# Layer 0 of a two-layer image network: another form for three small VectorE steps in the running maximum over k

## The chip, the cores and the metric

The kernel runs on one core of one Trainium2 chip. The metric is device time in microseconds of one execution, start to end; the median of 3 runs before the change is 9257.32 us (9255.66 to 9263.38). Five engines work side by side on a core, each through its own queue in order: TensorE (PE, with its weight loads shown apart as PEld), VectorE (DVE), ScalarE (ACT), GpSimd (POOL) and SyncE (SP), which here only issues DMAs. Working memory is SBUF, matmul results land in PSUM, both with 128 partitions.

## The reference, cut to what matters

Layer 0 is a linear attention over the pixels of each of 8 images (128 x 128 pixels, 128 channels, 4 heads of 32). Its softmax of k runs over the pixels, all 16384 of them, and so needs a maximum over the pixels for each channel:

```
qkv = einsum('bhwc,cf->bhwf', x, w_qkv);  q, k, v = split(qkv, 3, axis=-1)
q, k, v = (t.reshape(B, 4, 32, N) for t in (q, k, v))       # the raw reshape of the reference
q = softmax(q, axis=-2) * 32 ** -0.5
k = softmax(k, axis=-1)
context = einsum('bhdn,bhen->bhde', k, v)
attn = einsum('bhde,bhdn->bhen', context, q)
out = attn.reshape(B, H, W, 128) @ w_out + b_out
x = layernorm(out) * gamma + beta + x
```

Layer 1 (a gated projection, a depthwise convolution, and a selective scan in four directions) takes layer 0's output and is not touched.

## The kernel before, in words

Layer 0 takes the first 2100 us or so. An image lies in SBUF with channels on partitions. It is worked off in 32 groups of 4 x 128 pixels, and a step of the loop in `image` carries one group through every stage. Two images are in work at once: `attend(b)` computes the output of image b, while `context(b + 1)` builds the 128 x 128 context matrix of the next one. The order of the calls in `image` (the list of `at(stage, t - lag)` calls) is the order of instructions on every engine: the whole layer is built under `in_order`, which chains each instruction to the one before it on its engine. The first pass (b = -1) has only a context, the last (b = 7) only an attend.

The maximum is kept as a running one, as in a flash attention. Four groups make a block (BK = 4), so an image has 8 blocks, j = 0 to 7:

- `key` (L180, L182): PE computes k of a group as a [128 pixels of a column, 4 x 128 channels] tile, ACT copies it to `k`.
- `larger` (L186 to L197): DVE keeps the elementwise maximum of the block's four groups in `run` (L190, L192: one operand is in PSUM). At the block's last group two more operations fold the 4 columns of `run` into its first one (L196, L197: both operands in SBUF).
- `fold` (L199 to L214), one step later: PE turns the folded column (L206), DVE reduces it to the maximum per channel, `m` [128, 1] (L208). From the second block on, `m` is raised to the one before it (L210) and the difference `a` = old minus new is formed (L212). Then the diagonal matrix `dg` = ident x m is made (L214).
- `spread` (L219, L221): PE multiplies `ones` with `dg`, which puts the maxima on every partition in `pmx`; ACT takes exp of `a`.
- `subtract`, `raise_to`, `add`: k minus maximum (L231), exp (L234), and the product with v (L240), summed over a block in `pc`; L247 rescales `total` by `a` and adds the block.

Around these stand the stages of `attend`: on DVE the maxima of q (L270), the subtraction (L272), the sums (L280), their reciprocals (L281), the addition of the bias (L296) and the variance sums (L302); on POOL the multiplication of q (L282), three operations of the layer norm (L308, L310, L313) and the residual addition (L327); on ACT the activations L275, L290, L298, L325; on PE the matmuls L268, L288, L294, L321. Per step DVE's order is: L272, L231, L280, L281, then the block-end work of `fold` (L208 to L214) where it falls, then L190 or L192 with L196 and L197 where they fall, L296, L302, L270. POOL's is: L308, L310, L313, L327, L282.

The pools: `sm` holds the small tiles with 4 buffers, `wp` the group tiles with 2 unless said otherwise (`run` has 2), `ps` six PSUM banks.

Of the kernel before, what the change touches and what calls it, by code (L numbers as in the profile page):

```python
# [8 lines left out]
F32 = mybir.dt.float32  # L9
BF16 = mybir.dt.bfloat16  # L10
AF = mybir.ActivationFunctionType
ALU = mybir.AluOpType
AX = mybir.AxisListType
# [3 lines left out]
P = 128  # L17
# [60 lines left out]
def layer0(ctx: ExitStack, tc, xT, w_qkv, w_out, b_out, gamma, beta, win, x1, zs):  # L78
# [12 lines left out]
    nc = tc.nc  # L91
    const = ctx.enter_context(tc.tile_pool(name="l0c", bufs=1))
    wp = ctx.enter_context(tc.tile_pool(name="l0w", bufs=2))
    sm = ctx.enter_context(tc.tile_pool(name="l0s", bufs=4))
# [3 lines left out]
    ident = const.tile([P, P], F32, name="ident")  # L98
# [40 lines left out]
    def group(b, g):  # L139
        return xs[b % 2][:, g * GW : (g + 1) * GW, :]  # L140
# [33 lines left out]
    def context(b):  # L174

        ks, pks, ms, runs, scales = {}, {}, {}, {}, {}

        def key(g):
            pk = ps.tile([P, GW, P], F32, name="pk", tag="ps")
            nc.tensor.matmul(pk, wq[:, P : 2 * P], group(b, g), start=True, stop=True)  # L180
            ks[g] = k = wp.tile([P, GW, P], F32, name="k", tag="k", bufs=7)
            nc.scalar.copy(k, pk)  # L182
            pks[g] = pk

        def larger(g):
            pk = pks.pop(g)  # L186
            j, i = divmod(g, BK)
            if i == 1:
                runs[j] = run = wp.tile([P, GW, P], F32, name="run")
                nc.vector.tensor_tensor(run, pk, ks[g - 1], ALU.max)  # L190
            elif i > 1:
                nc.vector.tensor_tensor(runs[j], pk, runs[j], ALU.max)  # L192

            if i == BK - 1:
                run = runs[j]
                nc.vector.tensor_tensor(run[:, 0:2], run[:, 0:2], run[:, 2:4], ALU.max)  # L196
                nc.vector.tensor_tensor(run[:, 0], run[:, 0], run[:, 1], ALU.max)  # L197

        def fold(g):  # L199

            j, i = divmod(g, BK)
            if i < BK - 1:
                return
            run = runs.pop(j)
            turned = ps.tile([P, P], F32, name="pmt", tag="ps")
            nc.tensor.transpose(turned, run[:, 0, :], ident)  # L206
            ms[j] = m = sm.tile([P, 1], F32, name="m")
            nc.vector.tensor_reduce(m, turned, AX.X, ALU.max)  # L208
            if j:
                nc.vector.tensor_tensor(m, m, ms[j - 1], ALU.max)  # L210
                scales[j] = a = sm.tile([P, 1], F32, name="a")
                nc.vector.tensor_tensor(a, ms.pop(j - 1), m, ALU.subtract)  # L212
            runs[j] = dg = sm.tile([P, P], F32, name="dg", bufs=2)
            nc.vector.tensor_scalar(dg, ident, m, None, ALU.mult)  # L214

        def spread(g):
            j, i = divmod(g, BK)
            if i == BK - 1:
                nc.tensor.matmul(pm[:, j % 2, :], ones, runs.pop(j), start=True, stop=True)  # L219
                if j:  # L220
                    nc.scalar.activation(scales[j], scales[j], AF.Exp)  # L221

        def value(g):
            pv = ps.tile([P, GW, P], F32, name="pv", tag="ps")
            nc.tensor.matmul(pv, wq[:, 2 * P : 3 * P], group(b, g), start=True, stop=True)
            nc.scalar.copy(vts[g % 3][:, :, 0:P], pv)

        def subtract(g):

            mb = pm[:, g // BK % 2 : g // BK % 2 + 1, :]  # L230
            nc.vector.tensor_tensor(ks[g], ks[g], mb.to_broadcast([P, GW, P]), ALU.subtract)  # L231

        def raise_to(g):
            nc.scalar.activation(ks[g], ks[g], AF.Exp)  # L234

        def add(g):
            k = ks.pop(g)
            j, n = divmod(g, BK)
            for i in range(GW):
                nc.tensor.matmul(  # L240
                    pc, k[:, i, :], vts[g % 3][:, i, :],
                    start=(n == 0 and i == 0), stop=(n == BK - 1 and i == GW - 1),
                )
            if n < BK - 1:
                return
            if j:
                nc.vector.scalar_tensor_tensor(total, total, scales.pop(j), pc, ALU.mult, ALU.add)  # L247
            else:
                nc.vector.tensor_copy(total, pc)
            if g == NG - 1:  # L250
                rs = sm.tile([P, 1], F32, name="rs")
                nc.vector.reciprocal(rs, total[:, P : P + 1])
                for h in range(NH):
                    s = slice(HD * h, HD * h + HD)
                    nc.vector.tensor_scalar(
                        ctxs[b % 2][s, s], total[s, s], rs[s, :], HD**-0.5, ALU.mult, ALU.mult
                    )

        return key, larger, fold, spread, value, subtract, raise_to, add

    def attend(b):
# [1008 lines left out]
```

## Time and profile before

| what | before |
|---|---|
| median of 3 runs | 9257.32 us |
| the profiled execution, its own time | 9261.02 us |
| its span in the profile | 9259.2 us |
| layer 0, first context alone | about 0 to 110 us |
| layer 0, passes b = 0 to 6 (attend and context together) | about 110 to 2100 us |
| in 900 to 1200 us: PE busy | 276.63 us of 300 |
| in 900 to 1200 us: DVE busy | 209.68 us of 300 |
| in 900 to 1200 us: ACT, POOL busy | 179.65 us, 153.13 us of 300 |

A group in the profile is one line of the kernel on one engine: how often it ran, its total busy time, its mean duration, and the idle time of the engine just before it, with what ended that idle time. A line of a timeline gives start, duration, engine, source line and tiles of one instruction. A matmul in float32 is two passes in the records (x2). DVE's records may overlap by some 0.08 us[...].

### The profile page before, as it was taken

How to read it: one execution, taken by the hardware profiler on the slowest of the kernel's cores; microseconds unless marked ns; L12 is line 12 of the kernel's file. 1: busy time of each engine (PE TensorE's matmuls, PEld its weight loads, DVE VectorE, ACT ScalarE, POOL GpSimd, SP SyncE). 2: the span in 40 equal slices, each digit the busy share in tenths (PEclk: the TensorE clock that was granted, in tenths of full speed). 3: DMA queues.
4: the chain of work that ended last, by engine and by line, in shares of the span. 5: the costliest groups of instructions: out<-in, count | busy, mean ns of one | idle time of the engine just before them, and what ended most of it. 6: DMA issues, size and time to landing. Idle time of an engine off the chain costs nothing. (4 is left out here: it accounts for less than half of the span.)

```text
span 9259.2 us, 91316 instructions
## 1 busy us (share of the span) xinstructions
PE 6337.5 (68%) x24512; PEld 3096.6 (33%) x24512; DVE 7992.0 (86%) x7953; ACT 7099.7 (77%) x8066; POOL 7316.5 (79%) x4684
## 2 busy tenths in 40 slices
PE   8899998988899999999434636446364463643636
PEld 5555555554333333333101304114031140311403
DVE  6667666774699999999799999999999999999996
ACT  5555555657789999999688887887878888888885
POOL 3446444554588988888599899998999989999897
PEclk9999999999999999999655757557575575755857
DMA  1322333123478789888758769587695876957767
GB/s 76 146 84 96 137 121 146 70 109 137 148 242 249 251 246 244 245 246 241 206 154 238 208 185 258 158 230 216 179 260 159 222 225 178 257 165 218 230 174 211
DMA packets 934769, 1750.66 MB, mean 189 GB/s; under 512 B 150228, under 2 KB 376148, under 8 KB 926064
## 3 DMA queue, kind: packets, MB, share of 16 engines
q1 hardware_dynamic: 873328, 1509.92, 49.4%
q0 software_dynamic: 60928, 234.90, 13.8%
q8 instruction: 200, 3.28, 0.1%
q14 instruction: 313, 2.56, 0.1%
HBM read 1052.36 MB, written 692.12 MB: 188 GB/s over the span
## 5 line engine op out<-in xcount | busy, mean ns | idle before, releaser
L951 POOL TENSOR_TENSOR h<-ubt,sp 128x1024 f32<-128x1024 f32 x1024 | 2422.4, 2399 | 348.4 <-ACT mv L1058 124.1
L934 PE MATMUL px<-rows,dtw 128*128 128x512 bf16 x2048 | 953.5, 565 | 2266.2 <-DVE y L1001 1084.5
L534 DVE SCALAR_TENSOR_TENSOR acc<-xb,cw,acc 128x1024 f32<-128x1024 f32 x1024 | 1320.3, 1289 | 133.7 <-ACT xb L502 89.9
L526 POOL TENSOR_TENSOR tap<-tap 128x1024 f32<-128x1024 f32 x512 | 1224.0, 2394 | 243.9 <-ACT tap L524 220.6
L938 ACT ACTIVATE sp<-px 128x1024 f32<-128x1024 f32 x1024 | 1047.3, 1024 | 435.4 <-PE px L934 418.1
L961 DVE TENSOR_TENSOR_SCAN h<-px,h 128x1024 f32<-128x1024 f32 x512 | 1177.3, 2331 | 31.7 <-ACT px L942 15.1
L934 PEld LDWEIGHTS <-dtw 128*128 128x128 bf16 x2048 | 169.1, 110 | 3089.1 <-issue 1022.7
L959 DVE TENSOR_TENSOR_SCAN h<-px,h 128x1024 f32<-128x1024 f32 x512 | 1177.9, 2330 | 21.4 <-POOL h L951 18.8
L1009 POOL TENSOR_TENSOR y<-y,h 128x512 f32<-128x512 f32 x768 | 1159.8, 1559 | 3.8 <-DVE h L982 3.8
L942 ACT ACTIVATE px<-sp,sa 128x1024 f32<-128x1024 f32 x1024 | 1110.4, 1109 | 6.1
L515 PE MATMUL acc<-xi,wt 128*128 128x512 f32 x2048 | 938.3, 601 | 53.7 <-ACT ures L539 53.7
L524 ACT ACTIVATE tap<-xb,cw 128x1024 f32<-128x1024 f32 x768 | 837.3, 1139 | 15.2 <-POOL xb L499 15.1
L282 POOL TENSOR_TENSOR q<-q,qs 128x512 f32<-128x512 f32 x256 | 272.2, 1063 | 695.5 <-DVE qs L281 695.5
L938 ACT ACT_TABLE_LOAD x512 | 656.9, 1283 | 170.0 <-PE px L934 168.0
L942 ACT ACT_TABLE_LOAD x512 | 656.9, 1283 | 9.1
L1074 PEld LDWEIGHTS px<-wg,z 128*128 128x128 f32 x4096 | 575.3, 225 | 114.8 <-issue 109.1
L1074 PE MATMUL px<-wg,z 128*128 128x128 f32 x4096 | 574.7, 308 | 0.0
L967 PE MATMUL pc<-rows,csel 128*128 128x512 bf16 x1024 | 517.5, 586 | 78.2 <-DVE rstd L1062 74.5
L515 PEld LDWEIGHTS acc<-xi,wt 128*128 128x128 f32 x2048 | 375.1, 189 | 574.4 <-issue 411.9
L488 PE MATMUL pxb<-xi,wi 128*128 128x512 f32 x1024 | 496.2, 607 | 2.1 <-ACT xb L497 2.1
L298 ACT ACTIVATE sq<-o 128x512 f32<-128x512 f32 x256 | 161.2, 630 | 421.0 <-DVE o L296 419.8
L1001 DVE TENSOR_TENSOR y<-y,px 128x1024 f32<-128x1024 f32 x384 | 468.6, 1220 | 14.4
(153 smaller groups left out, 15038.8 us busy)
## 6 DMA issues: line engine op xcount, KB each, us to landing
ubt<-ubs SPq DMA_DIRECT2D x1024, 512.0 KB
zs<-z SPq DMA_DIRECT2D x512, 256.0 KB
ubs<-ures SPq DMA_DIRECT2D x256, 512.0 KB
ubs<-turned SPq DMA_DIRECT2D x256, 512.0 KB
z<-zs SPq DMA_DIRECT2D x256, 512.0 KB
y<-gs POOLq DMA_DIRECT2D x128, 1024.0 KB, 10.3
gs<-du POOLq DMA_DIRECT2D x96, 1024.0 KB, 8.6
rows<-xps SPq DMA_DIRECT2D x1536, 60.0 KB
```

Source lines behind the costliest of these rows:

```text
L515: nc.tensor.matmul(acc[:, s, :], wt[:, j, c, :], x, start=(j == 0), stop=(j == len(ON_PE) - 1))
L524: nc.scalar.activation(t, at(n, c, *d), AF.Copy, scale=weight(n, c, *d))
L526: nc.gpsimd.tensor_tensor(sums[n, c], sums[n, c], t, ALU.add)
L534: nc.vector.scalar_tensor_tensor(acc, at(n, c, *d), weight(n, c, *d), acc, ALU.mult, ALU.add)
L934: nc.tensor.matmul(p[:, hf * 512 : hf * 512 + 512], sl.dw[:, c * P : c * P + P], src, start=True, stop=True)
L938: nc.scalar.activation(t, da[n, c], AF.Softplus)
L942: nc.scalar.activation(da[n, c], sp[n, c], AF.Exp, scale=sa[:, sl.s, c : c + 1])
L951: nc.gpsimd.tensor_tensor(h, u, t, ALU.mult)
L959: nc.vector.tensor_tensor_scan(e[:, ::-1], x[:, ::-1], e[:, ::-1], start, ALU.mult, ALU.add)
L961: nc.vector.tensor_tensor_scan(e, x, e, start, ALU.mult, ALU.add)
L1009: nc.gpsimd.tensor_tensor(v[:, c], v[:, c], h[:, c], ALU.add)
L1074: nc.tensor.matmul(po[:, w, :], z[:, c, w * H : w * H + H], wg[:, c, :], start=(c == 0), stop=(c == NC2 - 1))
```

## The change

The two tensor operations at the end of `larger` become one reduction over the four columns: it reads `run` in the order "p h w", so that the four values to be compared lie 128 elements (512 bytes) apart, and writes a tile of its own, `top`. The transposition in `fold` then reads `top`. The maximum and the difference of `fold` become tensor-scalar operations, whose second operand is the [128, 1] tile taken as a scalar per partition; the values are the same.

```diff
             if i == BK - 1:
                 run = runs[j]
-                nc.vector.tensor_tensor(run[:, 0:2], run[:, 0:2], run[:, 2:4], ALU.max)
-                nc.vector.tensor_tensor(run[:, 0], run[:, 0], run[:, 1], ALU.max)
+                runs[j] = top = sm.tile([P, P], F32, name="top", bufs=2)
+                nc.vector.tensor_reduce(top, run.rearrange("p w h -> p h w"), AX.X, ALU.max)
 
         def fold(g):
...
-            run = runs.pop(j)
+            top = runs.pop(j)
             turned = ps.tile([P, P], F32, name="pmt", tag="ps")
-            nc.tensor.transpose(turned, run[:, 0, :], ident)
+            nc.tensor.transpose(turned, top, ident)
             ms[j] = m = sm.tile([P, 1], F32, name="m")
             nc.vector.tensor_reduce(m, turned, AX.X, ALU.max)
             if j:
-                nc.vector.tensor_tensor(m, m, ms[j - 1], ALU.max)
+                nc.vector.tensor_scalar(m, m, ms[j - 1], None, ALU.max)
                 scales[j] = a = sm.tile([P, 1], F32, name="a")
-                nc.vector.tensor_tensor(a, ms.pop(j - 1), m, ALU.subtract)
+                nc.vector.tensor_scalar(a, ms.pop(j - 1), m, None, ALU.subtract)
             runs[j] = dg = sm.tile([P, P], F32, name="dg", bufs=2)
             nc.vector.tensor_scalar(dg, ident, m, None, ALU.mult)
```

## The prediction

> **What bounds the kernel now.** I read the page first: the span, the engines' shares, and the slices. Layer 0 is the first nine of the 40 slices.
>
> ```profile
> span 9259.2 us, 91316 instructions
> ...
> PE   8899998988899999999434636446364463643636
> ...
> DVE  6667666774699999999799999999999999999996
> ```
>
> PE is nearly full there and DVE far from it, so time comes off only where PE stands idle, and DVE counts where PE waits for it. The list of waits between 100 and 2100 us has, as PE's longest wait for another engine's arithmetic:
>
> ```profile
> PE pmx L219 <- DVE dg L214: 49.0, 46, 1.3
> ```
>
> PE waits for `dg`, the last product of the fold that is changed, about 1.07 us in each of 46 cases. Next, the instructions of the tiles `run` and `m` (minimum/median/maximum in ns):
>
> ```profile
> L196 DVE TENSOR_TENSOR run<-run x64: 424/1140/1516, 22.2 to 2081.1; 128x256 f32<-128x256 f32 x64
> L197 DVE TENSOR_TENSOR run<-run x64: 291/292/1020, 22.6 to 2082.7; 128x128 f32<-128x128 f32 x64
> ```
> ```profile
> L208 DVE TENSOR_REDUCE m<-pmt x64: 227/228/291, 23.4 to 2085.6; 128x1 f32<-128x128 f32 x64
> L214 DVE TENSOR_SCALAR dg<-ident,m x64: 272/274/570, 23.8 to 2086.2; 128x128 f32<-128x128 f32 x64
> L210 DVE TENSOR_TENSOR m<-m x56: 158/504/514, 33.7 to 2085.9; 128x1 f32<-128x1 f32 x56
> L212 DVE TENSOR_TENSOR a<-m x56: 158/970/972, 33.9 to 2086.1; 128x1 f32<-128x1 f32 x56
> ```
>
> An operation on one element per partition takes 158 ns or 970. The timelines of DVE, POOL and PE around one fold show what makes the difference:
>
> ```profile
> 1054.31 0.23 DVE L208 TENSOR_REDUCE m<-pmt 128x1 f32<-128x128 f32 x1
> 1054.57 0.50 DVE L210 TENSOR_TENSOR m<-m 128x1 f32<-128x1 f32 x1
> 1055.11 0.97 DVE L212 TENSOR_TENSOR a<-m 128x1 f32<-128x1 f32 x1
> 1056.00 0.28 DVE L214 TENSOR_SCALAR dg<-ident,m 128x128 f32<-128x128 f32 x1
> 1056.20 0.68 DVE L296 TENSOR_TENSOR o<-po,bb 128x512 f32<-128x512 f32 x1
> ```
> ```profile
> 1053.79 1.27 POOL L327 TENSOR_TENSOR x<-x1t,x 128x512 f32<-128x512 f32 x1
> 1055.01 1.05 POOL L282 TENSOR_TENSOR q<-q,qs 128x512 f32<-128x512 f32 x1
> ```
> ```profile
> 1053.88 1.16 PE L321 MATMUL pt<-d,o 128*128 128x128 f32 x8
> 1056.33 0.49 PE L219 MATMUL pmx<-dg,ones 128*128 128x128 f32 x2 [1.28 <-DVE dg L214]
> ```
>
> L210 ends with POOL's L327 (1055.07 against 1055.06), L212 with L282 (1056.08 against 1056.06). While these hold DVE, PE idles. L196 does the same a step earlier: it starts 0.19 us after an L282 and ends after it.
>
> [...] L196 to L212 wait, while the SBUF reduction L280 has a mean of 686 ns beside the same POOL work. [...] no row here shows a one-element tensor-scalar. L214 (128 elements, source in SBUF) [...] in first blocks, where it follows L208 directly, it takes 570 ns.
>
> **The change part by part.**
>
> *Folding the columns.* Out go L196 and L197. In 48 of the 56 blocks with POOL at work, L196's start to L296's start is 1.38 to 1.41 us, in each image's last block 1.75, so I take 1.39. In comes a reduction of 512 elements. Contiguous it would be 0.69 us (L280). But its reads hop 512 bytes at each element. The nearest row hops the same way:
>
> ```profile
> L152 DVE COPY v<-x x192: 637/749/1566, 341.5 to 1867.0; 128x512 f32<-128x512 f32 x192
> ```
>
> [...] L296 starts 0.08 us before the end of the operation ahead of it, at 1.06. Gain 0.33 per block (bounds 0.04 and 0.78). In the first pass POOL is idle and the pair takes 0.75 us together; the reduction loses 0.4 there, 8 times, beside PE's own matmuls: nothing to 3 us.
>
> *Maximum and difference.* 42 folds (blocks 1 to 6 of 7 passes) have both blocked; block 0 has neither, block 7 finds POOL free. A tensor-scalar with a pointer: [...] 0.206 us for one element (bounds 0.158, the tensor form, and 0.215). From L208's start: maximum at 0.26 to 0.47, difference (a gap of 0.04, as between L210 and L212) at 0.51 to 0.71, L214 0.08 before its end, at 0.63. [...] L327's record ends at 0.75, L282's begins at 0.70. [...] Each image's first block has a like case: L196 starts at 1022.78, L282 at 1022.84, and L196 runs its full-speed 0.42 while L282 stretches to 1.28. So 0.06 us ahead is enough; 0.19 behind isn't. L214 would be 0.07 ahead[...]. I take that L214 wins: end at 0.90, L296 at 0.83 instead of 1.89, a gain of 1.06 per fold. If it loses, [...] L296 at 1.76: a gain of 0.13. In block 7 and the first pass the fold becomes 0.1 longer (14 times, 1 us at most).
>
> *Other edits.* `top` instead of `run` for the transposition: same size, its step comes later than the fold, PE waited 2.9 us in all for it. `run` is free earlier; nobody waits for it. No DMA and no queue is moved.
>
> **The sum.** Starts of L196 are 26.16 us apart in most blocks (1414.19, 1440.35, 1466.51). DVE's saving there would be 0.33 + 1.06 = 1.39. But PE sets a floor: its query matmuls are 6.12 us apart in steps without a fold (1056.65, 1062.77), so a block takes 4 x 6.12, plus 0.11 for the transposition and 0.32 for L219: 24.91. So at most 1.25 per block is saved, and what is late next is PE itself. 42 x 1.25 = 52.5; blocks 0 and 7 give about 0.25 each, 14 x 0.25 = 3.5. Sum 56 us. The profiled execution took 9261.02 (span 9259.2), 3.7 above the median of 9257.32; from the median, 9257.3 - 56 = 9201. Layer 1 has the same instructions.
>
> **The rivals.**
>
> *A, forecast: L214 gets in before L282.* 9201. With the reduction at its dear end 1.10 per block remain: 46 + 1, so 9210; with all at its best the floor holds at about 9196.
>
> *B: L214 loses to L282.* The wait moves from L212 to L214. 42 x (0.33 + 0.13) + 3.5 = 23, so 9234; with the reduction at either bound 9248 to 9216. For it: the near tie. Against it: the 0.06 us case.
>
> *C: the change doesn't do what it says, since the one-element forms wait too.* L210 and L212 stay as long as before. 42 x 0.33 + 3.5 = 17, so 9240. For it: tensor-scalars of 128 elements wait, and no row shows one element. [...]
>
> *D, slower: the strided reduction costs more than what it replaces.* With B holding too, it decides from 1.39 + 0.08 + 0.13 = 1.60 us on, 2.8 ns per hop. [...] 2.15 us, 42 x 0.55 + 14 x 0.6 = 31 us slower, 9288. Against it: [...] the reductions L280 and L302 cost the same 686 ns with rows of 32 and of 128, so short rows add nothing visible.
>
> **How the numbers follow.** A 0.55, B 0.23, C 0.15, D 0.07. About 0.2% (18.5 us) is what a measurement of this kernel can tell from no change. A is faster by more; of B and C, at 23 and 17 us, about half: 0.19. So faster 0.74, within 0.2% 0.19, slower 0.07. The range reaches from A's best, with some of PE's remaining waits for POOL's `d` taken too, 9190, over B and C to 9246.
>
> **What would show it.** The reduction's row: 1.14 us, the same with and without POOL at work. L210 and L212: about 0.21 in all 56. L214: 0.27 with L282 stretched (A), or about 1.2 (B). PE's wait for `dg` nearly gone (A) or about 0.5 to 0.8 per fold (B, C). Distance of blocks: 24.9 (A), 25.7 (B), 25.8 (C), over 26.2 (D). I am wrong if the one-element forms wait, if the hop costs over 2.8 ns, or if PE turns out to have a floor above 24.9.

## The result and the profile after

The median after is 9187.98 us (9182.95 to 9194.06), against 9256.49 before in the runs that were taken beside it: 68.5 us less, ratio 0.9926 with a 95% interval of 0.9914 to 0.9939. That is faster, as forecast, but the forecast was 9201 (56 us less), and the time lies 2 us below the range of 9190 to 9246.

The page of the changed kernel, with the same lines as before:

```profile
span 9182.9 us, 91090 instructions
...
PE   8999999998899999999334536345363463643636
...
DVE  6667666673899999999799999999999999999996
```

PE's slices of layer 0 read 9 more often, DVE's hardly changed: what went away was idle time of PE. PE's list of waits from 100 to 2100 us (total, cases, longest) has the old wait nearly at the end:

```profile
PE pt L321 <- POOL d L313: 30.9, 32, 1.9
...
PE pmx L219 <- DVE dg L214: 0.6, 4, 0.2
```

49.0 us before, 0.6 now. The wait for POOL's `d`, at the starts of the images, is now the longest on arithmetic. The instructions that write `top` and `m` (minimum/median/maximum, ns; first that of `top`, then, from the view of the other tile, those of `m`):

```profile
L197 DVE TENSOR_REDUCE top<-run x64: 1018/1056/1072, 23.1 to 2013.1; 128x128 f32<-128x512 f32 x64
```
```profile
L208 DVE TENSOR_REDUCE m<-pmt x64: 226/228/292, 24.6 to 2016.8; 128x1 f32<-128x128 f32 x64
L214 DVE TENSOR_SCALAR dg<-ident,m x64: 274/277/568, 25.0 to 2017.5; 128x128 f32<-128x128 f32 x64
L210 DVE TENSOR_SCALAR m<-m x56: 211/214/216, 35.2 to 2017.1; 128x1 f32<-128x1 f32 x56
L212 DVE TENSOR_SCALAR a<-m x56: 211/214/215, 35.5 to 2017.3; 128x1 f32<-128x1 f32 x56
```

None of the three new forms waits anywhere, with POOL at work or without: minimum and maximum lie 4 to 54 ns apart. One fold on the timelines of DVE and POOL:

```profile
1050.57 0.23 DVE L208 TENSOR_REDUCE m<-pmt 128x1 f32<-128x128 f32 x1
1050.83 0.21 DVE L210 TENSOR_SCALAR m<-m 128x1 f32<-128x1 f32 x1
1051.08 0.21 DVE L212 TENSOR_SCALAR a<-m 128x1 f32<-128x1 f32 x1
1051.21 0.27 DVE L214 TENSOR_SCALAR dg<-ident,m 128x128 f32<-128x128 f32 x1
1051.40 0.68 DVE L296 TENSOR_TENSOR o<-po,bb 128x512 f32<-128x512 f32 x1
```
```profile
1050.04 1.28 POOL L327 TENSOR_TENSOR x<-x1t,x 128x512 f32<-128x512 f32 x1
1051.27 1.12 POOL L282 TENSOR_TENSOR q<-q,qs 128x512 f32<-128x512 f32 x1
```

`dg` starts 0.06 us before L282 and runs unhindered; L282 takes 1.12 us instead of 1.05, longer by 0.07 us. L296 follows L208 after 0.83 us, where it was 1.89. So in all 42 folds.

The time can be followed step by step on DVE by the distance from one variance sum (L302) to the next, the median over the 7 passes, in us:

| step | before | after |
|---|---|---|
| with the column fold, blocks 1 to 6 | 7.39 | 6.98 to 7.08 |
| with the rest of the fold (next step) | 6.99 | 5.94 |
| each of the two others | 5.89 | 5.89 |
| column fold of block 0 | 7.16 | 6.72 |
| column fold of block 7 | 6.45 | 5.67 |

For example, the step with the rest of a fold, before and then after (6.99 and 5.94 us apart):

```profile
1077.08 0.69 DVE L302 TENSOR_REDUCE var<-sq 128x4 f32<-128x512 f32 x1 [0.76 <-ACT sq L298]
1084.07 0.69 DVE L302 TENSOR_REDUCE var<-sq 128x4 f32<-128x512 f32 x1 [0.76 <-ACT sq L298]
```
```profile
1046.90 0.69 DVE L302 TENSOR_REDUCE var<-sq 128x4 f32<-128x512 f32 x1 [0.76 <-ACT sq L298]
1052.84 0.69 DVE L302 TENSOR_REDUCE var<-sq 128x4 f32<-128x512 f32 x1 [0.76 <-ACT sq L298]
```

A pass from its first L302 to its last takes 199.5 us before and 189.8 after (sum of the seven: 68.2 us less). The first L302 of all comes 2.2 us later (122.5 to 124.7: the first pass got longer), and the stretches between passes add up to 2.7 less. The last L302 starts at 2084.4 before and 2015.6 after: 68.8 us, the whole result. The profiled executions differ by 76.3 us (9261.02 and 9184.71), 7.5 more than layer 0 gives. What follows layer 0 has the same instructions in all kernels here, yet in their profiled executions it took from 7167 to 7187 us. So below, "end of layer 0" is the start of the last L302 (or of the same instruction under a shifted line number), and small effects are read from it.

### The profile page after: what moved, and what is told of

It is laid out like the page before. It is cut to its first block, busy times and chain, and to the rows that moved or that the text cites. A ratio compares the mean times of both kernels' runs of the same rounds, so it can differ in the third digit from the quotient of the medians.

```text
span 9182.9 us, 91090 instructions
## 1 busy us (share of the span) xinstructions
PE 6273.2 (68%) x24350; PEld 3080.2 (34%) x24512; DVE 7929.7 (86%) x7889; ACT 7102.3 (77%) x8066; POOL 7317.2 (80%) x4684
## 5 line engine op out<-in xcount | busy, mean ns | idle before, releaser
L934 PE MATMUL px<-rows,dtw 128*128 128x512 bf16 x1893 | 909.9, 573 | 2302.7 <-DVE y L1001 1084.5
L282 POOL TENSOR_TENSOR q<-q,qs 128x512 f32<-128x512 f32 x256 | 273.0, 1066 | 694.6 <-DVE qs L281 691.1
L938 ACT ACT_TABLE_LOAD x512 | 656.9, 1283 | 169.5 <-PE px L934 122.8
L982 DVE TENSOR_TENSOR h<-h,pc 128x1024 f32<-128x1024 f32 x384 | 466.0, 1214 | 0.0
```

The costliest lines, as they stand in the source:

```text
L934: nc.tensor.matmul(p[:, hf * 512 : hf * 512 + 512], sl.dw[:, c * P : c * P + P], src, start=True, stop=True)
L938: nc.scalar.activation(t, da[n, c], AF.Softplus)
```

## The experiments

Each ratio is against the kernel before, run beside the experiment: a median of 9261.09 us for the first four, 9258.69 for the last four.

**The scalars alone.**

```diff
-                nc.vector.tensor_tensor(m, m, ms[j - 1], ALU.max)
+                nc.vector.tensor_scalar(m, m, ms[j - 1], None, ALU.max)
...
-                nc.vector.tensor_tensor(a, ms.pop(j - 1), m, ALU.subtract)
+                nc.vector.tensor_scalar(a, ms.pop(j - 1), m, None, ALU.subtract)
```

> The two tensor operations that fold the columns (L196, L197) stay as they were; only the maximum and the difference take a per-partition scalar. My account: each of the 42 folds beside POOL's work saves 1.05 us (L208 to L296: 1.89 before, 0.84 after), DVE stays the bound at about 26.16 - 1.05 = 25.1 us per block, layer 0 gets 44 us shorter: about 9212. Rival (PE's floor of 24.8 already takes part of it, or the saving only counts together with the reduction): under 35 us saved, over 9222. L282 should be stretched to 1.12 us in these folds, as in the changed kernel.

Measured: 9216.12, ratio 0.9953 (0.9938 to 0.9968), 45 us less. End of layer 0 at 2042.1, 42.3 us earlier. The step with the fold goes from 6.99 to 5.94, the one with the column fold stays at 7.39. A block is 25.11 us long, as the account has it (25.1). The saving stands alone, at the size of the account.

**The reduction alone.**

```diff
+                runs[j] = top = sm.tile([P, P], F32, name="top", bufs=2)
+                nc.vector.tensor_reduce(top, run.rearrange("p w h -> p h w"), AX.X, ALU.max)
...
                 nc.vector.tensor_tensor(m, m, ms[j - 1], ALU.max)
...
```

> Only the column fold becomes one strided reduction; maximum and difference stay tensor operations with two SBUF operands. My account: 0.42 us saved in each of 49 blocks and 0.77 in the last block of each of 7 passes, 26 us, less 3.2 us lost in the first pass where POOL is idle: about 23 us saved, 9233. L210 and L212 stay at 0.50 and 0.97 us. If this and the run with the scalars alone add up to the 68 us of the whole change, the two parts are independent; if they add up to more, PE's floor eats the rest in the whole change; if to less, each part needs the other.

Measured: 9234.38, ratio 0.9970 (0.9958 to 0.9983), 27 us less; end of layer 0 at 2057.2, 27.2 earlier. The tensor forms wait as before:

```profile
L210 DVE TENSOR_TENSOR m<-m x56: 158/501/511, 35.3 to 2058.8; 128x1 f32<-128x1 f32 x56
L212 DVE TENSOR_TENSOR a<-m x56: 158/970/972, 35.5 to 2058.9; 128x1 f32<-128x1 f32 x56
```

The seven passes are 25.8 us shorter here and 44.2 with the scalars alone, 70.0 together; in the whole change they are 68.2 shorter. The parts are nearly independent: PE's floor takes away 1.8 us, not the 6 that the prediction let it take (42 blocks at 1.25 instead of 1.39).

**A tiny operation ahead of `dg`.**

```diff
+            gap = sm.tile([P, 1], F32, name="gap")
+            nc.vector.memset(gap, 0.0)
             nc.vector.tensor_scalar(dg, ident, m, None, ALU.mult)
```

> The changed kernel with one more small DVE operation (a memset of a [128, 1] tile, about 60 ns) between the difference and dg, so that dg starts at about 0.70 us from L208's start instead of 0.64, about where L282 starts. Theory [...]: dg loses to L282 in some or all of 42 folds, its duration goes from 0.28 to 1.1 us, and the time rises by up to 42 x 0.9 = 38 us, to about 9226. Rival [...]: dg stays at 0.28, L282 is stretched to 1.12, and the time stays within 3 us of the changed kernel, 9188 to 9191.

Measured: 9224.12, ratio 0.9958 (0.9943 to 0.9973); end of layer 0 at 2044.5, 28.9 us later than in the changed kernel. The memset didn't push `dg` back by its 59 ns; it runs beside it, and `dg`'s record starts at 0.65 instead of 0.64. Yet most folds now lose. Two folds of this kernel on DVE, the second of them lost (`dg` is L216 here):

```profile
221.09 0.21 DVE L212 TENSOR_SCALAR a<-m 128x1 f32<-128x1 f32 x1
221.23 0.28 DVE L216 TENSOR_SCALAR dg<-ident,m 128x128 f32<-128x128 f32 x1
221.26 0.06 DVE L215 MEMSET gap<- 128x1 f32 x1
...
246.16 0.21 DVE L212 TENSOR_SCALAR a<-m 128x1 f32<-128x1 f32 x1
246.30 1.19 DVE L216 TENSOR_SCALAR dg<-ident,m 128x128 f32<-128x128 f32 x1
246.32 0.06 DVE L215 MEMSET gap<- 128x1 f32 x1
```

And the POOL operations that they meet (L282 of the other kernels):

```profile
221.29 1.13 POOL L284 TENSOR_TENSOR q<-q,qs 128x512 f32<-128x512 f32 x1
...
246.35 1.05 POOL L284 TENSOR_TENSOR q<-q,qs 128x512 f32<-128x512 f32 x1
```

Either `dg` is at full speed (0.28 us) and POOL's operation stretched (1.13), or POOL's takes its 1.05 us and `dg`, at 1.19, ends 0.09 us after it. By the trace 30 of the 42 are lost, and 12 won. The records can't tell beforehand which: `dg` starts 0.05 to 0.07 us ahead of POOL's operation in both. A lost fold brings the bias addition (L296 of the other kernels) 0.91 us later (1.76 against 0.85 from L208; the prediction had 1.76 for a loss): 30 x 0.91 = 27 us, nearly all of the 28.9. So what rival B describes does happen. How near the changed kernel is to it can only be estimated: where `dg` wins here, L284 takes 1.13 us on average, 0.01 more than L282 in the changed kernel, so `dg` holds POOL up some 0.01 us longer. That such a delay alone tips the 30 folds, and not something else that the memset does, isn't shown.

**Two elements instead of one.**

```diff
-            ms[j] = m = sm.tile([P, 1], F32, name="m")
-            nc.vector.tensor_reduce(m, turned, AX.X, ALU.max)
+            ms[j] = m = sm.tile([P, 2], F32, name="m")
+            nc.vector.tensor_reduce(m, turned.rearrange("p (o c) -> p o c", o=2), AX.X, ALU.max)
...
-                nc.vector.tensor_scalar(m, m, ms[j - 1], None, ALU.max)
+                nc.vector.tensor_scalar(m, m, ms[j - 1][:, 0:1], None, ALU.max)
...
+                a = sm.tile([P, 2], F32, name="a")
...
+                nc.vector.tensor_scalar(a, ms.pop(j - 1), m[:, 0:1], None, ALU.subtract)
...
```

> The changed kernel with m and a two elements wide: the reduction of L208 leaves the maxima of the two halves of the pixels apart, the maximum and the difference work on both columns, and only the first column is used, so the subtracted value is a maximum over half of the pixels (the softmax doesn't depend on which value is subtracted). Theory [...]: L210 rises from 0.21 to about 0.5 and L212 to about 1.0 us beside POOL's work, and the time goes back to that of the reduction alone, about 9233. Rival (a tensor-scalar this small never waits): L210 and L212 stay at 0.21 us and the time at 9188.

Measured: 9236.13, ratio 0.9973 (0.9962 to 0.9984); end of layer 0 at 2058.3, within 1.1 us of the reduction alone. The difference is L213 here:

```profile
L210 DVE TENSOR_SCALAR m<-m x56: 228/508/520, 35.2 to 2059.8; 128x2 f32<-128x2 f32 x56
L213 DVE TENSOR_SCALAR a<-m x56: 227/968/971, 35.5 to 2060.1; 128x2 f32<-128x2 f32 x56
```

With one more element per partition the tensor-scalars wait just as the tensor forms did, 508 and 968 ns, and the scalars' whole gain is gone. Rival C had fallen with the 214 ns of the changed kernel; this run shows that it was the single element that made it fall. One element doesn't wait, 214 ns in all 56 cases within 3 ns; two do. Why the two differ, no run shows.

**A reduction with contiguous reads.**

```diff
-                nc.vector.tensor_reduce(top, run.rearrange("p w h -> p h w"), AX.X, ALU.max)
+                nc.vector.tensor_reduce(top, run.rearrange("p w (h o) -> p (w h) o", o=GW), AX.X, ALU.max)
```

> The changed kernel, but the reduction takes the maximum over four neighbouring channels in place of the four columns, so that its reads are contiguous; the subtracted value is then not the channel's maximum (the softmax doesn't depend on which value it is). Theory 1 (PE is the floor of the changed kernel, 3 x 6.12 + 6.44 = 24.79 us a block): the reduction falls from 1.06 to about 0.69 us, but the blocks stay at 24.7 to 24.8, only blocks 0 and 7 and the first pass gain, about 5 us in all: 9183. Rival (DVE still sets the pace): 0.37 us in each of 56 blocks and 0.3 in each of 8 of the first pass, about 23 us: 9165.

Measured: 9177.1, ratio 0.9916 (0.9902 to 0.9929), 13 us under the changed kernel beside it (9190.22); end of layer 0 at 2002.8, 12.8 and 15.2 earlier than in the two profiles of the changed kernel. That is between the two expectations, so the steps must tell. The reduction takes 0.69 us:

```profile
L197 DVE TENSOR_REDUCE top<-run x64: 685/686/687, 22.5 to 2000.6; 128x128 f32<-128x512 f32 x64
```

DVE's steps in blocks 3 and on are 6.83, 5.94, 5.90 and 6.12: the step without any fold has grown from 5.89 to 6.12, since DVE now waits. The query matmuls of PE there:

```profile
1116.55 1.02 PE L268 MATMUL pq<-x,wq 128*128 128x512 f32 x2
...
1122.66 1.02 PE L268 MATMUL pq<-x,wq 128*128 128x512 f32 x2
...
1128.78 1.02 PE L268 MATMUL pq<-x,wq 128*128 128x512 f32 x2
...
1134.89 1.02 PE L268 MATMUL pq<-x,wq 128*128 128x512 f32 x2
...
1141.34 1.02 PE L268 MATMUL pq<-x,wq 128*128 128x512 f32 x2
```

6.11, 6.12, 6.11 and 6.45: 24.79 us a block, the distance that the changed kernel reaches in its later blocks too. And PE is what sets it: in the changed kernel PE waits for nothing at all from 1090 to 1160 us. The floor of theory 1 stands at its number; its guess of 5 us was too small. The gain lies elsewhere: 8.5 us within the seven passes, in their blocks 0 to 2, where DVE isn't yet held up by PE, and in block 7 (5.67 to 5.36); 2.4 in the first pass; 1.9 between passes.

**The old pair in the first pass.**

```diff
+                if b == 0:
+                    nc.vector.tensor_tensor(run[:, 0:2], run[:, 0:2], run[:, 2:4], ALU.max)
+                    nc.vector.tensor_tensor(run[:, 0], run[:, 0], run[:, 1], ALU.max)
+                    return
                 runs[j] = top = sm.tile([P, P], F32, name="top", bufs=2)
...
```

> The changed kernel, with the old pair of tensor operations for the column fold in the first pass alone, where POOL is idle (0.75 us for both against 1.06). Theory: the first pass goes back from 113.4 to 110.2 us, all else stays: 3 us faster than the changed kernel, 9185, which the profile can show and the times hardly. Rival (the first pass is longer because of the tensor-scalars in the fold, 0.06 us each): it stays at 113 us.

Measured: 9193.83, ratio 0.9930 (0.9918 to 0.9943). The first context is written at 111.5 us, against 110.2 before, 113.4 in the changed kernel and 114.4 in its repetition. So 2 to 3 us of the first pass come from the reduction. The expected return to 110.2 wasn't reached; the run with the scalars alone has the same first pass as this one and writes at 110.1, so 1.4 us lie within what two executions differ by. The scalars have no visible share: with them alone the first L302 starts at 122.4, before at 122.5, here at 122.8, in the changed kernel at 124.7. The times don't show the gain; as a version it isn't proven better.

**The difference after `dg`.**

```diff
-                scales[j] = a = sm.tile([P, 1], F32, name="a")
-                nc.vector.tensor_scalar(a, ms.pop(j - 1), m, None, ALU.subtract)
             runs[j] = dg = sm.tile([P, P], F32, name="dg", bufs=2)
             nc.vector.tensor_scalar(dg, ident, m, None, ALU.mult)
+            if j:
+                scales[j] = a = sm.tile([P, 1], F32, name="a")
+                nc.vector.tensor_scalar(a, ms.pop(j - 1), m, None, ALU.subtract)
```

> The changed kernel with the difference issued after dg instead of before it. Theory (order of requests decides): dg starts at 0.52 us from L208's start instead of 0.64, [...] ends at about 0.83, in all 42 folds ahead of L282; PE sees dg 0.07 us earlier, DVE goes on to L296 about 0.1 us later than in the changed kernel. As PE is the floor, the time stays within 5 us of the changed kernel. Rival (DVE sets the pace): 42 x 0.1 = 4 us slower and block distances of 24.8 in blocks 1 and 2 too, 24.9 later.

Measured: 9196.53, ratio 0.9934 (0.9920 to 0.9947); end of layer 0 at 2016.2, with 2015.6 and 2017.9 in the two profiles of the changed kernel. One fold (`dg` is L212, the difference L215, the bias addition L297):

```profile
1100.06 0.23 DVE L208 TENSOR_REDUCE m<-pmt 128x1 f32<-128x128 f32 x1
1100.33 0.21 DVE L210 TENSOR_SCALAR m<-m 128x1 f32<-128x1 f32 x1
1100.57 0.32 DVE L212 TENSOR_SCALAR dg<-ident,m 128x128 f32<-128x128 f32 x1
1100.81 0.20 DVE L215 TENSOR_SCALAR a<-m 128x1 f32<-128x1 f32 x1
1100.94 0.67 DVE L297 TENSOR_TENSOR o<-po,bb 128x512 f32<-128x512 f32 x1
```

`dg` is 0.13 us further ahead of POOL's next operation, takes 0.04 to 0.05 us longer, ends 0.07 to 0.10 us after the one before (L328 here), and gets in between the two in all 42 folds; L297 follows L208 after 0.88 instead of 0.84. The passes keep their length (1328.6 us in sum, 1328.5 and 1328.8 in the changed kernel). The time is 6 us above that of the changed kernel beside it, just over the 5 that were expected, but layer 0 has no part in that. So this order costs nothing in layer 0 that these runs can show, and has three times the lead.

**The changed kernel again.**

> The changed kernel again, beside the others on one chip: dg ahead of L282 in all 42 folds (0.28 us each), 68 us below the kernel before, block distances 24.7 to 24.8. If dg's lead over L282 is down to chance, some folds lose here and dg takes 1.2 us in them.

Measured: 9190.22, ratio 0.9927 (0.9913 to 0.9940), 68.5 us less again; `dg` takes 0.28 us in all 42 folds. The lead is small, but the same from fold to fold and from execution to execution.

## Why the prediction came out as it did

The reading was right in each part. The waits of L196, L210 and L212 were waits for POOL's operations: in all 42 folds of the kernel before, L210 ends 13 to 20 ns after L327 and L212 14 to 18 ns after L282. The new forms don't wait (L210 and L212 take 211 to 216 ns now), `dg` gets in before L282, and PE's wait for `dg` goes (49.0 us, then 0.6). That one element per partition wouldn't wait, and would take 0.206 us (it takes 0.214), was assumed: no row of the kernel before shows either. But that `dg` wins was in part luck: the prediction's case for it, *"So 0.06 us ahead is enough"*, doesn't hold as a rule, since with the memset a mean lead of 0.056 us lost 30 of 42 times. A fold saves 1.05 us (forecast 1.06). What failed is the size of the sum, 56 us for 68, and its terms were these:

- *"But PE sets a floor ... 24.91. So at most 1.25 per block is saved".* This is the step that failed. The 0.32 us for L219 was read behind a wait, from its start at 1056.33 to the next matmul of the kernel before:

```profile
1056.65 1.02 PE L268 MATMUL pq<-x,wq 128*128 128x512 f32 x2
```

  In an unbroken stream of the changed kernel it is 0.22:

```profile
1149.91 1.06 PE L321 MATMUL pt<-d,o 128*128 128x128 f32 x8
1150.80 0.39 PE L219 MATMUL pmx<-dg,ones 128*128 128x128 f32 x2
1151.02 1.02 PE L268 MATMUL pq<-x,wq 128*128 128x512 f32 x2
```

  That is no single case: 0.32 or 0.33 in all 49 folds with L268 next before, 0.22 in 32 of the 49 after. With it the floor is 24.79 to 24.80, as the contiguous reduction shows. Nor does it bind DVE from the start: by L302 the first blocks of a pass come out below it, at 24.70, where DVE still keeps its own pace and catches up with PE, whose query matmuls are never less than 24.79 us a block apart. Blocks 1 to 6 saved 1.43 us each on average, not 1.25: 7.5 us over 42 blocks, of which the lower floor makes 5 (42 x 0.12).
- *"blocks 0 and 7 give about 0.25 each".* Their column folds gave 0.44 and 0.78. In block 7 the pair had waited for L327, 1.75 us in all, which the prediction noted and then left out of the sum: 1.3 + 3.6 = 5 us over the seven passes.
- *"The reduction's row: 1.14 us".* It is 1.06. No row of the kernel before shows what a hop costs, on which the 1.14 rests, and with it the small end of the gain (0.04), the dear end (1.10 per block) and D's 2.15 us. The runs show it: contiguous the reduction takes 0.69, so by an estimate from the medians a hop of 512 bytes costs (1056 - 686) / 512 = 0.72 ns more per element. The cheaper reduction made the saving per column fold 0.41 to 0.44 instead of 0.33; under the floor it counts in part.
- *The first pass, "nothing to 3 us".* 2 to 4 us longer, at or over the end of that bound: PE waits 5.3 us for `top` there, where it waited 2.9 for `run`.
- Between passes 2.7 us came off that the prediction hadn't; other kernels scatter by as much there (the sum of the six stretches is 560 to 567 us), so this stays open.

The range's lower end rested on the same floor and so failed with it. The chances given to B and C weren't idle: B was some 0.01 us away by the estimate above, and C one element.

## What to carry to other kernels

Where a tiny VectorE operation has two very different durations (158 and 970 ns here), set it beside GpSimd's timeline: it may be waiting for an operation there to end. In these runs operations with two SBUF operands did (L196, L197, L210, L212: up to 1516, 1020, 514 and 972 ns), and tensor-scalars on more than one element per partition (968 ns on 2, 1.19 us on 128); tensor-scalars on one (211 to 216 ns) and the reduction in SBUF (1018 to 1072 ns) did not. A form that doesn't wait is worth far more than its own length if TensorE waits behind it: 1.05 us a fold here, for two operations of 214 ns. Where the gain hangs on which engine asks first, find out by how much, and reorder for a lead; a lead of 0.06 us between two records was not safe here, one of 0.19 was won in all 42 folds. And take an instruction's share of a floor from a stretch in which nothing waits: behind a wait it cost more here (0.32 us against 0.22), and a floor that is 0.1 us too high hides gain in every block.

## What the runs showed of the hardware that was not expected

- Which of the two engines goes first can't be read from the starts in the records: `dg`, 0.052 to 0.069 us ahead of L282 in the changed kernel (mean 0.062), wins 42 of 42; with a memset beside it, 0.049 to 0.066 us ahead (mean 0.056), it loses 30 of 42. Losing cost DVE 0.91 us a fold; being beaten cost POOL 0.07.
- The memset, 59 ns by its own record, delayed a `dg` that won by 0.02 us at most: its record lies inside that of `dg`, which comes after it in the queue.
- A one-element tensor-scalar with a pointer took 214 ns where the tensor form took 158 unhindered. On two elements it took 228 unhindered.
